# Perceiver layer on one core: the second batch's keys later, one of its head groups in the last cross-attention unit, the last batch's projections one step earlier

## The chip, the cores and the metric

The kernel runs on one core of one Trainium2 chip. The metric is the device time of one execution in microseconds (us). TensorE is called PE here, VectorE DVE, ScalarE ACT, GpSimd POOL, and SyncE, which only issues DMAs, SP.

## What is computed

One layer with three parts, each added to its input `x` of shape (4 batches, 256 tokens, 256): cross-attention to a context of 4096 tokens, causal linear attention over the 256 tokens, and a gated feed-forward network. Biases are left out here:

```python
x = x + cross_attention(layernorm(x), ctx)      # 16 heads of 16, softmax over 4096 keys
x = x + linear_attention(layernorm(x))
x = x + ffn(layernorm(x))

def linear_attention(x):
    q, k, v = split(x @ Wqkv)                   # 16 heads of 16
    qf, kf = features(q), features(k)           # 64 features of a head
    out_t = sum_{s<=t} (qf_t . kf_s) v_s / sum_{s<=t} (qf_t . kf_s)
    return out @ Wout

def features(v):                                # v divided by its norm, then random features
    return exp(clip(omega v/|v| * sqrt(2s) - s, -20, 20)) * weight

def ffn(x):
    return (silu(x @ wg.T) * (x @ wu.T)) @ wd.T
```

Everything is fp32.

## The kernel before

**Cross-attention** (`cross_attention`, L664 to L1137) walks through 16 units, one for each batch and each quad of four heads, and each unit through 16 steps of 256 context tokens. A step `n` issues the score products of its own four heads (`pt`, L845, then the exponentials on ACT, L850), the products of a unit ahead from which the row maxima are taken (`pm` L799, reduced on DVE at L806), then extra pieces of work, and last the value product of step `n - 1` (`pav`, L865), which DVE adds up in `av` (L873, L875). The loop is at L1102. The maxima run 19 steps ahead, so they end in step -4, counted from the first step of the last unit; the key and value projections of the context end before that. In the last unit only `pt`, `pav` and extra pieces are left.

**The extra pieces** come from `plan` (L482), a table by hand. Its keys are steps counted from the start of the last unit: -60 to 11. It holds the causal attention of batches 0, 1 and 2 up to their scaled queries and keys, and the attention of batch 0. `qk_normed(t)` (L277) multiplies the queries and keys of token tile `t` by their inverse norms on DVE. `qk_turned(t)` (L281) turns them with four PE transposes, and DVE copies the result to `qkT`. `features(n)` (L293) makes the features of quads `n` and `n + 1`: PE products `pf` into four PSUM banks, four clamps on DVE (L307), four exponentials on ACT (L308), four scalings on POOL (L309). `normalised` (L158) is a layer norm on DVE alone, 18 instructions for two tiles.

**A quad of the causal attention** is `attend(n)` (L313), three functions called at different places. `scores`: products `pa` (L327, L332) into four banks; two of the four results go to SBUF through an ACT copy (L338) and a POOL select that zeroes the upper triangle (L339), the other two through a DVE product with a mask (L344). `values`: products `po` (L353), copied by ACT (L358). `divide`: for two quads together, PE transposes `pt_o` (L365), then three DVE instructions. Quads 0 to 3 are batch 0, 4 to 7 batch 1, and so on. `output(b)` is the projection after it: transposes `tr_o`, ACT copies, products `py` (L397), DVE adds into `xr` (L398).

**The tail** is the loop over quads at L651. In step `n` it issues `values` of quad `n - 1`, `scores` of quad `n`, `divide` in even steps, `features` where `early` says so, and then `fills[n]`, lists by hand (L594 to L648). The fills hold the feed-forward (`feed_forward`, L536: `turn`, `hidden(0..2)` with the products `pg`, `pu`, and `down` with `pd`) of batch 0 in steps 4 to 8 and of batch 1 from step 9, the end of cross-attention (`divide15`, `project15`), and the causal preparation of batch 3: `norm3`, `turn3`, `qk3` (products `pqk`, DVE add, POOL square), `sq3` (DVE reduce), `v3` (products `pv`, DVE adds), `ends` (the inverse norms, 13 small DVE instructions in five pieces), `qk_normed(6)`, `qk_normed(7)`, `qk_turned(6)`, `qk_turned(7)` and `features(12)`. `begin(1)` is the layer norm of batch 1's feed-forward. `divide15` needs DMAs that `finish(15)` issues on SP after the last `av` (L886 to L904).

**The order** on PE, ACT, DVE and SP is the order of the calls (`manual_schedule`, L591 and L981): each engine works off its own list in turn and waits at its head. All PSUM results come from one ring of eight banks (`bank`, L201), taken in the order of the calls; a product waits until the reader of the result eight allocations ago is done.

Of the kernel before, what the change touches and what calls it, by code (L numbers as in the profile page):

```python
# [12 lines left out]
F32 = mybir.dt.float32  # L13
# [7 lines left out]
P = 128  # L21
B, T, D = 4, 256, 256
# [4 lines left out]
NQ = H // 4  # L27
# [12 lines left out]
def perceiver_layer(  # L40
# [5 lines left out]
    nc = tc.nc  # L46
# [150 lines left out]
    lnp = ctx.enter_context(tc.tile_pool(name="lnp", bufs=2))  # L197
# [79 lines left out]
    def qk_normed(t):  # L277
        to = qk[t].rearrange("p (h d) -> p h d", d=HD)
        nc.vector.tensor_tensor(to, to, nrm[:, t, :].unsqueeze(2).to_broadcast([P, 2 * H, HD]), ALU.mult)

    def qk_turned(t):  # L281
        ps = bank([P, 4, P], "tr_qk")
        for k in range(4):
            nc.tensor.transpose(ps[:, k, :], qk[t][:, k * P : (k + 1) * P], ident)
        nc.vector.tensor_copy(qkT[:, :, t * P : (t + 1) * P], ps)
# [24 lines left out]

    got, place = [], {}

    def attend(n):  # L313

        b, q = divmod(n, NQ)
        ats = []

        def scores():  # L320
            for part in range(2):
                f = feature(n, part)
                qf, kf = f[:, :T], f[:, T:]
                pas = [bank([P, 3, P], "pa") for _ in range(2)]
                for j, pa in enumerate(pas):
                    rows = slice(64 * j, 64 * j + 64)
                    nc.tensor.matmul(  # L327
                        pa[:, 0:2, :], lhsT=kf[rows, :P], rhs=qf[rows, :], start=True, stop=True
                    )
                for j, pa in enumerate(pas):  # L330
                    rows = slice(64 * j, 64 * j + 64)
                    nc.tensor.matmul(  # L332
                        pa[:, 2, :], lhsT=kf[rows, P:], rhs=qf[rows, P:], start=True, stop=True
                    )
                for pa in pas:
                    at = place["at"]()
                    if part == 0:
                        nc.scalar.copy(at, pa)  # L338
                        nc.gpsimd.affine_select(  # L339
                            out=at[:, 0:3:2, :], in_=at[:, 0:3:2, :], compare_op=ALU.is_ge, fill=0.0, base=0,  # L340
                            pattern=[[0, 2], [1, P]], channel_multiplier=-1,
                        )
                    else:
                        nc.vector.tensor_tensor(at, pa, place["mask"], ALU.mult)  # L344
                    ats.append(at)

        def values():
            po = bank([P, T], "po")
            for i in range(2):
                for j, at in enumerate(ats):  # L350
                    c0 = (4 * q + j) * (HD + 1)
                    rhs = at[:, 2, :] if i else at[:, 0:2, :]
                    nc.tensor.matmul(  # L353
                        po[32 * j : 32 * j + 32, i * P : T], lhsT=va[:, 2 * b + i, c0 : c0 + 32], rhs=rhs,
                        start=i == 0, stop=i == 1,
                    )
            oT = place["avT"]()
            nc.scalar.copy(oT, po)  # L358
            got.append(oT)

        def divide():
            pt = bank([P, 2, 8, 32], "pt_o")
            for m, oT in enumerate(got):
                for i in range(2):
                    nc.tensor.transpose(  # L365
                        pt[:, i, 4 * m : 4 * m + 4].rearrange("p j r -> p (j r)"), oT[:, i * P : (i + 1) * P], ident
                    )
            got.clear()
            den = lnp.tile([P, 2, 8], F32, tag="den", name="den")
            nc.vector.tensor_scalar(den, pt[:, :, :, HD], 1e-6, None, ALU.max)  # L370
            nc.vector.reciprocal(den, den)
            nc.vector.tensor_tensor(
                place["att"](b)[:, :, 64 * q - 64 : 64 * q + 64].rearrange("p t (j d) -> p t j d", d=HD),
                pt[:, :, :, :HD], den.unsqueeze(3).to_broadcast([P, 2, 8, HD]), ALU.mult,
            )

        return scores, values, divide
# [54 lines left out]
    def start_causal():  # L432
# [3 lines left out]
        n = 2 * (B - 1)  # L436
# [39 lines left out]
        def call(f, *args):  # L476
            return lambda: f(*args)

        steps = [attend(n) for n in range(NQ)]
        turn_o, project_o = output(0)  # L480
        z0 = lnp.tile([P, 2, D], F32, tag="z1", name="z1", bufs=4)
        plan = {  # L482
# [11 lines left out]
            -13: [call(qk_normed, 0)], -12: [call(qk_normed, 1)],  # L494
            -11: [call(qk_turned, 0)], -10: [call(qk_turned, 1)],
            -7: [call(weight_load, n) for n in range(6)],
            -6: [call(qk_normed, 2)], -5: [call(qk_normed, 3)],
            -4: [call(qk_turned, 2), call(qk_turned, 3), call(weight, 0)],
            -3: [call(features, 0)],
            -2: [call(weight, 1)],  # L500
            -1: [steps[0][0], call(weight, 2)],
            0: [steps[0][1], steps[1][0]],
            1: [call(features, 2)],
            2: [steps[1][1], call(weight, 3), call(qk_normed, 4)],
            3: [steps[1][2], steps[2][0]],
            4: [steps[2][1], steps[3][0]],
            5: [call(weight, 4), call(qk_normed, 5)],
            6: [steps[3][1], call(qk_turned, 4), call(qk_turned, 5)],
            7: [steps[3][2], call(weight, 5)],
            8: [turn_o],  # L510
            9: [call(features, 4)],
            10: [project_o],
            11: [call(normalised, lambda t: z0[:, t, :], (0, 1))],
        }

        for b, at in enumerate((-18, -11, -3)):
# [74 lines left out]
    with tc.manual_schedule(engines={ET.PE, ET.Activation, ET.DVE, ET.SP}):  # L591
        *divide15, project15 = finish
        NB = B * NQ
        fills = {n: [] for n in range(NB + 1)}  # L594
        norm3, turn3, qk3, sq3, v3, _ = causal_in(3)
        ff = {0: feed_forward(0)}

        def call(b, part, *args):
            return lambda: ff[b][part](*args)

        def begin(b):
            ff[b] = feed_forward(b)
            ff[b][0]()

        def outputs(b):
            for piece in output(b):
                piece()


        fills[4] += [call(0, 1)]  # L610
        for m in range(NH // 2):
            fills[5 + m] += [call(0, 2, m)]
        fills[8] += [call(0, 3, i) for i in range(2)]

        fills[6] += divide15
        fills[7] += [project15, norm3]
        turn_o, project_o = output(1)
        fills[8] += [turn_o, turn3, project_o, lambda: begin(1), lambda: qk3(0)]
        ends = normed_pieces((6, 7))
        fills[9] += [lambda: qk3(1), lambda: sq3(0), v3, lambda: sq3(1), *ends[:2]]  # L620
        fills[10] += ends[2:]

        for b in range(1, B):
            n0 = 4 * b + 4
            turn, down = call(b, 1), [call(b, 3, i) for i in range(2)]
            hidden = [call(b, 2, m) for m in range(NH // 2)]
            if b > 1:
                fills[n0] += [lambda b=b: outputs(b)]
                if b == B - 1:
                    fills[n0] += [lambda: nc.scalar.activation(spare, eps, AF.Sqrt)]  # L630
                fills[n0] += [lambda b=b: begin(b)]
            if b < B - 1:
                fills[n0 + 1] += [turn]
                fills[n0 + 2] += [hidden[0]]
            if b < B - 2:
                fills[n0 + 3] += [hidden[1]]
                fills[n0 + 4] += [hidden[2]]
                fills[n0 + 5] += down
            elif b == B - 2:
                fills[n0 + 3] += [hidden[1]]  # L640
                ends = [hidden[2]] + down
            else:
                fills[n0][:0] = ends[:1]
                split = [call(B - 2, 3, 1, parts) for parts in (range(3), range(3, NH))]
                fills[n0] += ends[1:2] + split[:1] + [turn] + split[1:] + hidden + down
        fills[4] += [lambda: features(6)]
        fills[10] += [lambda: qk_normed(6), lambda: qk_normed(7)]
        fills[11] += [lambda: qk_turned(6), lambda: qk_turned(7), lambda: features(12)]  # L648
        early = {6: 8, 8: 10, 13: 14}
        steps = [attend(n) for n in range(NB)]  # L650
        for n in range(NQ, NB + 1):  # L651
            if n > NQ:
                steps[n - 1][1]()
            if n < NB:
                steps[n][0]()
            if n > NQ and n % 2 == 0:
                steps[n - 1][2]()
            if n in early:
                features(early[n])
            for piece in fills[n]:  # L660
                piece()
# [550 lines left out]
```

## Time and profile before

| | us |
|---|---|
| median of 3 runs (1192.37 to 1193.15) | 1193.06 |
| the profiled execution, its own time | 1193.6 |
| its span, first to last instruction | 1191.9 |
| last product of cross-attention starts / the tail's first product | 1064.02 / 1067.26 |
| PE busy, share of the span | 1176.9, 99% |
| DVE busy, share of the span | 912.3, 77% |
| ACT busy, share of the span | 690.7, 58% |

The busy time of PE contains the time that a product stands at the head of its queue with its ends modelled, so 99% does not mean that PE never waits. The waits are read from the chain of work that ended last, and from the idle times ahead of the weight loads (PEld), which stop when PE waits. All times below are us from the start of the span. The last unit begins at 1014.23 (`pt` of step 0).

### The profile page before, as it was taken

To read this page: it belongs to the slowest core of one execution; us is meant where nothing else is said; L and a number is where in the kernel's file an instruction comes from. 1 tells how busy PE (TensorE), PEld (TensorE's weight loads), DVE (VectorE), ACT (ScalarE), POOL (GpSimd) and SP (SyncE) were. 2 spreads that over 40 slices of the span, in tenths; PEclk is the share of its full clock that TensorE was granted. 3 is DMA by queue.
4 is the path that set the end of the run, shared out by engine and by line. 5 is a ranking of instruction groups with operands and counts; after the bars stand their busy time and mean duration, and the time that the engine had idled before them with its cause. 6 is when DMAs were issued, how large, how long until landed. Compare 5 with 4: busy or idle time off the path is not lost.

```text
span 1191.9 us, 43006 instructions
## 1 busy us (share of the span) xinstructions
PE 1176.9 (99%) x18024; PEld 800.7 (67%) x18024; DVE 912.3 (77%) x1756; ACT 690.7 (58%) x1435; POOL 232.5 (20%) x439
## 2 busy tenths in 40 slices
PE   8999999999999999999999999999999999999998
PEld 4476667666776677667766776677666566667677
DVE  7987777877777777877787878798887788557753
ACT  4446666666666666666666666665664446884332
POOL 3730302020211112121212020203021121113210
PEclk8999999999999999999999999999999999999999
DMA  6572432244223322343224322432243120000000
GB/s 209 139 213 72 108 117 81 63 111 118 81 66 96 111 92 83 86 116 94 73 78 117 97 82 77 116 105 73 79 104 89 56 65 28 11 8 9 6 10 18
DMA packets 55161, 100.00 MB, mean 84 GB/s; under 512 B 23392, under 2 KB 28056, under 8 KB 54968
## 3 DMA queue, kind: packets, MB, share of 16 engines
q1 hardware_dynamic: 44904, 91.84, 26.6%
q0 software_dynamic: 9440, 4.81, 2.2%
q8 instruction: 143, 2.34, 0.8%
q10 hardware_dynamic: 624, 0.59, 0.2%
q14 instruction: 50, 0.41, 0.1%
HBM read 76.13 MB, written 3.21 MB: 67 GB/s over the span
## 4 chain that ended last, share of the span: by engine, by line
PE 96%; DVE 2%; ACT 1%; DMA 0%; issue 0%; ACTq 0%; POOL 0%; DVEq 0%
PE pt L845 23%; PE pm L799 19%; PE pav L865 19%; PE pv L180 11%; PE pk L180 11%; PE pg L564 2%; PE pu L564 2%; PE pd L580 1%; PE pa L327 1%; PE pqk L180 1%; DVE mx L806 1%; PE po L353 1%; PE py L397 1%; PE pf L301 1%; PE py L180 1%; PE pa L332 1%
## 5 line engine op out<-in xcount | busy, mean ns | idle before, releaser
L850 ACT ACTIVATE e<-pt 128x512 f32<-128x512 f32 x1024 | 529.8, 602 | 374.0 <-PE pm L799 360.0
L806 DVE TENSOR_REDUCE mx<-pm 128x1 f32<-128x512 f32 x1024 | 634.9, 683 | 124.7 <-PE pm L799 124.4
L845 PE MATMUL pt<-qa,kt 32*128 32x256 f32 x4096 | 504.1, 388 | 0.9 <-DVE qa L831 0.5
L799 PE MATMUL pm<-kt,qT 32*128 32x512 f32 x2048 | 501.9, 617 | 0.1
L845 PEld LDWEIGHTS pt<-qa,kt 32*128 32x128 f32 x4096 | 319.3, 184 | 124.3 <-ACT v L770 41.6
L865 PE MATMUL pav<-e,v 128*32 128x256 f32 x4096 | 269.9, 380 | 0.0
L799 PEld LDWEIGHTS pm<-kt,qT 32*128 32x128 f32 x2048 | 183.2, 191 | 17.6 <-DVE mx L806 4.9
L865 PEld LDWEIGHTS pav<-e,v 128*32 128x32 f32 x4096 | 128.7, 110 | 76.1 <-issue 5.6
L875 DVE TENSOR_TENSOR av<-pav,av 128x256 f32<-128x256 f32 x240 | 101.6, 423 | 62.2 <-PE pav L865 61.9
L180 PE MATMUL pv<-wv_sb,wff 128*32 128x128 f32 x4096 | 137.3, 276 | 0.0
L180 PE MATMUL pk<-wff,wk_sb 128*32 128x256 f32 x2048 | 137.1, 389 | 0.0
L180 PEld LDWEIGHTS pv<-wv_sb,wff 128*32 128x32 f32 x4096 | 104.3, 109 | 43.9 <-DVE mx L806 43.9
L180 PEld LDWEIGHTS pk<-wff,wk_sb 128*32 128x32 f32 x2048 | 54.7, 110 | 66.6 <-DVE mx L806 38.8
L914 POOL TENSOR_TENSOR oT<-oT,bvT 128x64 f32<-128x64 f32 x32 | 8.6, 289 | 391.0 <-DVE oT L911 391.0
L897 POOL DMA_DIRECT2D oT<-scr x112 | 66.5, 623 | 21.3 <-DMA scr<-av 18.3
L742 ACT ACTIVATE ku<-pk,bk_sb 128x256 f32<-128x256 f32 x128 | 63.2, 495 | 12.6 <-PE pk L180 11.1
L821 POOL DMA_DIRECT2D qa<-neg x60 | 33.0, 559 | 141.5 <-DVE neg L818 104.4
L770 ACT COPY v<-pv 128x256 f32<-128x256 f32 x128 | 51.3, 401 | 9.7 <-PE pv L180 9.7
L308 ACT ACTIVATE kt<-kt,shift 128x512 f32<-128x512 f32 x32 | 22.3, 727 | 18.1 <-DVE kt L307 18.1
L972 POOL DMA_DIRECT2D qT<-qu x56 | 26.9, 488 | 15.3 <-ACT qu L969 10.7
L344 DVE TENSOR_TENSOR at<-pa,mask 128x384 f32<-128x384 f32 x32 | 16.3, 551 | 16.0 <-PE pa L332 15.9
L307 DVE TENSOR_SCALAR kt<-pf,low,top 128x512 f32<-128x512 f32 x32 | 23.7, 803 | 5.0 <-PE pf L301 5.0
(143 smaller groups left out, 646.0 us busy)
## 6 DMA issues: line engine op xcount, KB each, us to landing
wff<-in_ctxT_dram SPq DMA_DIRECT2D x128, 512.0 KB
kt<-ku SPq DMA_DIRECT2D x510, 32.0 KB
scr<-av POOLq DMA_DIRECT2D x14, 128.0 KB, 2.0
oT<-scr POOLq DMA_DIRECT2D x112, 8.0 KB, 2.5
xr<-in_x_dram SPq DMA_DIRECT2D x4, 256.0 KB
out_dram<-o SPq DMA_DIRECT2D x8, 128.0 KB
qa<-neg POOLq DMA_DIRECT2D x60, 1.0 KB, 3.4
qT<-qu POOLq DMA_DIRECT2D x56, 16.0 KB, 3.8
```

What stands on the lines that cost most here:

```text
L180: nc.tensor.matmul(out[js], lhsT=lhsT[:, js], rhs=rhs, **flags)
L564: nc.tensor.matmul(ps[:, i, :], lhsT=w[:, k, ns], rhs=zT[:, k, :], start=k == 0, stop=k == KC - 1)
L742: nc.scalar.activation(ku[:, cs], made.pop(), AF.Identity, bias=bk_sb[:, m : m + 1])
L770: nc.scalar.copy(to.rearrange("p t (h d) -> p t h d", d=HD + 1)[:, :, :, :HD], made.pop().rearrange("p t (h d) -> p t h d", d=HD),)
L799: nc.tensor.matmul(pm, lhsT=qT[rows, q, ts], rhs=kt[rows, c * CH : (c + 1) * CH], start=True, stop=True,)
L806: nc.vector.tensor_reduce(mx[:, i, j, c : c + 1], pm, AX.X, ALU.max)
L821: nc.gpsimd.dma_start(out=qa[32 * j : 32 * j + 1, :].rearrange("o (p i) -> o p i", i=2), in_=neg[:, j, :])
L845: nc.tensor.matmul(pt[:, i, :], lhsT=kt[rows, ks], rhs=qa[rows, :], start=True, stop=True)
L850: nc.scalar.activation(e, pt, AF.Exp, scale=0.25)
L865: nc.tensor.matmul(pav[32 * h : 32 * h + 32, :], lhsT=v[:, t % KT, c0 : c0 + 32], rhs=es[n, h][:, i, :], start=i == 0, stop=i == 1,)
L875: nc.vector.tensor_tensor(avs[u], pav, avs[u], ALU.add)
L897: queue.dma_start(out=oT[:, k, q % 2, j], in_=scr[32 * j : 32 * j + HD, k * P : (k + 1) * P].rearrange("e (r a) -> r e a", a=16),)
```

## The change

It does four things. (1) In `plan`, `qk_normed` and `qk_turned` of tiles 2 and 3 (batch 1) leave steps -6 to -4 and take the places that tiles 4 and 5 (batch 2) had in steps 2, 5 and 6; tiles 4 and 5 go to steps 8, 11, 13 and 14. (2) Quad 4, the first of batch 1, has its `scores` in step 12 and its `values` in step 15 of the last unit and not in steps 4 and 5 of the tail; with `scalar=False` all four of its results go through DVE's mask, and DVE copies its `po` into a tile of its own. (3) `divide15` goes ahead of `divide` of quads 4 and 5 in step 6, `project15` and `norm3` from step 7 to step 6, `turn3` from 8 to 7, `qk3` from 8 and 9 to 8 alone, with the first ahead of `down` and the second ahead of `project_o`, and `ends` all to step 9. (4) `qk_turned(6)` goes to the end of step 10, and `qk_turned(7)` and `features(12)` go ahead of `hidden(1)` of batch 1 in step 11.

```diff
-    def attend(n):
+    def attend(n, scalar=True):
...
-                    if part == 0:
+                    if part == 0 and scalar:
                         nc.scalar.copy(at, pa)
...
                     else:
                         nc.vector.tensor_tensor(at, pa, place["mask"], ALU.mult)
...
-            oT = place["avT"]()
-            nc.scalar.copy(oT, po)
+            if scalar:
+                oT = place["avT"]()
+                nc.scalar.copy(oT, po)
+            else:
+                oT = lnp.tile([P, T], F32, tag="avT4", name="avT4", bufs=1)
+                nc.vector.tensor_copy(oT, po)
             got.append(oT)
...
-        steps = [attend(n) for n in range(NQ)]
+        steps, step4 = [attend(n) for n in range(NQ)], attend(NQ, False)
...
-            -6: [call(qk_normed, 2)], -5: [call(qk_normed, 3)],
-            -4: [call(qk_turned, 2), call(qk_turned, 3), call(weight, 0)],
+            -4: [call(weight, 0)],
...
-            2: [steps[1][1], call(weight, 3), call(qk_normed, 4)],
+            2: [steps[1][1], call(weight, 3), call(qk_normed, 2)],
...
-            5: [call(weight, 4), call(qk_normed, 5)],
-            6: [steps[3][1], call(qk_turned, 4), call(qk_turned, 5)],
+            5: [call(weight, 4), call(qk_normed, 3)],
+            6: [steps[3][1], call(qk_turned, 2), call(qk_turned, 3)],
             7: [steps[3][2], call(weight, 5)],
-            8: [turn_o],
+            8: [turn_o, call(qk_normed, 4)],
             9: [call(features, 4)],
             10: [project_o],
-            11: [call(normalised, lambda t: z0[:, t, :], (0, 1))],
+            11: [call(normalised, lambda t: z0[:, t, :], (0, 1)), call(qk_turned, 4)],
+            12: [step4[0]],
+            13: [call(qk_normed, 5)],
+            14: [call(qk_turned, 5)],
+            15: [step4[1]],
...
-        fills[6] += divide15
-        fills[7] += [project15, norm3]
+        first = {6: divide15}
+        fills[6] += [project15, norm3]
+        fills[7] += [turn3]
         turn_o, project_o = output(1)
-        fills[8] += [turn_o, turn3, project_o, lambda: begin(1), lambda: qk3(0)]
+        fills[8][:0] = [lambda: qk3(0)]
+        fills[8] += [turn_o, lambda: qk3(1), project_o, lambda: begin(1), lambda: sq3(0)]
         ends = normed_pieces((6, 7))
-        fills[9] += [lambda: qk3(1), lambda: sq3(0), v3, lambda: sq3(1), *ends[:2]]
-        fills[10] += ends[2:]
+        fills[9] += [v3, lambda: sq3(1), *ends]
...
-        fills[10] += [lambda: qk_normed(6), lambda: qk_normed(7)]
-        fills[11] += [lambda: qk_turned(6), lambda: qk_turned(7), lambda: features(12)]
+        fills[10] += [lambda: qk_normed(6), lambda: qk_normed(7), lambda: qk_turned(6)]
+        fills[11][:0] = [lambda: qk_turned(7), lambda: features(12)]
...
         for n in range(NQ, NB + 1):
-            if n > NQ:
+            if n > NQ + 1:
                 steps[n - 1][1]()
-            if n < NB:
+            if NQ < n < NB:
                 steps[n][0]()
+            for piece in first.get(n, []):
+                piece()
             if n > NQ and n % 2 == 0:
                 steps[n - 1][2]()
```

## The prediction

> **What bounds the kernel now.** I read the chain of waits first: 96% of it is PE, so work taken off PE or waits ahead of PE decide. Then the busy times of the stretches that the edits touch:
>
> ```profile
> 985.00:1002.33 17.33, 17.33 (x196) 10.30 (x193) 16.84 (x37) 10.43 (x20) 0.54 (x2) 1.00 0.15 48
> ...
> 1014.23:1051.00 36.77, 36.77 (x503) 23.97 (x503) 18.91 (x43) 32.12 (x66) 6.03 (x14) 1.00 0.05 9
> 1051.00:1067.26 16.26, 15.91 (x199) 8.56 (x198) 7.95 (x30) 13.13 (x26) 1.69 (x5) 1.00 0.01 3
> ...
> 1104.20:1131.20 27.00, 24.40 (x256) 17.14 (x248) 21.62 (x59) 8.38 (x17) 5.92 (x11) 1.00 0.01 2
> ```
>
> The columns after the length are PE, PEld, DVE, ACT, POOL, granted clock (1.00 throughout). Unit 14 (first row) is DVE's: 16.84 of 17.33. The last unit is PE's with ACT close behind. In the tail's middle (last row) DVE is busy for 21.62 of 27.00 and PE is short of work for some of it. So the change moves DVE work out of a stretch that DVE bounds, PE work from the tail into the last unit, and reorders a stretch in which PE and DVE take turns.
>
> **Unit 14: the pieces that leave.** The timeline there:
>
> ```profile
> 995.65 0.68 DVE L279 TENSOR_TENSOR kt<-kt,nrm 128x512 f32<-128x512 f32 x1
> 996.25 0.41 DVE L875 TENSOR_TENSOR av<-pav,av 128x256 f32<-128x256 f32 x1
> ...
> 999.18 0.68 DVE L279 TENSOR_TENSOR kt<-kt,nrm 128x512 f32<-128x512 f32 x1
> ...
> 1001.31 1.09 PE L284 MATMUL tr_qk<-ident,kt 128*128 128x128 f32 x8
> ...
> 1002.50 1.27 DVE L285 COPY qT<-tr_qk 128x512 f32<-128x512 f32 x2
> 1003.70 0.41 DVE L875 TENSOR_TENSOR av<-pav,av 128x256 f32<-128x256 f32 x1
> ```
>
> Start to start, the two scalings hold DVE for 0.60 each and the copies for 1.20: 2.40, and DVE has no idle time there. PE loses 1.0 of transposes. A step cannot fall below what PE needs: `pav` starts at 984.10 and 987.02, 2.92 apart, in the step without extras. The steps -5 and -4 now last 3.73 and 4.55 (`pav` at 994.05, 997.78, 1002.33). Following the queues, `pav` of -5 comes 0.60 earlier (DVE), that of -4 3.0 after it, at 1000.2 for 1002.33: **-2.1**. Ends: -0.9 if PE sets the pace in spite of the busy DVE, -2.4 if all of DVE's time is won. The new row maximum of the last unit comes earlier by as much, so its four POOL DMAs (issued from 1005.56) still land ahead of 1014.23 as they do now. Steps 2, 5 and 6 get tiles 2 and 3 for tiles 4 and 5, the same instructions: nothing.
>
> **The last unit: what is added.** PE: two `qk_turned` of 0.59, `scores` 1.51 (1032.37 to 1033.88), `values` 0.79 (1031.59 to 1032.37): 3.48. DVE: two scalings 0.68, two copies 0.69, four masks of 0.51, one copy of 0.42 (as L873): 5.2. ACT gets nothing. In the end of the unit PE waits twice:
>
> ```profile
> 1058.41 0.34 DVE av L875
> 1058.76 0.04 issue
> 1058.80 1.13 PE pt L845 x12
> 1059.94 1.00 PE pav L865 x16
> ...
> 1064.09 3.25 PE pav L865 x32
> ```
>
> `pt` of step 13 (first four at 1057.75, the rest at 1058.80) waits 1.05 for the bank that `av` frees behind `normalised`; the last two `pav`, 1.0 each, take 3.25: 1.25 of waiting for ACT. Now step by step. `qk_normed(4)` in step 8 falls in 2.24 of DVE idle ahead of 1046.24: free. In step 11 `qk_turned(4)` takes 0.59 of PE, and its copy goes behind `normalised`, to 1059.0. In step 12 PE reaches the second half of `scores` at 1057.95; its two banks are the ones of that copy and of step 11's `av` (1059.35), so it waits 1.1. The masks behind run to 1061.4; `pt` of step 13 needs the first one's bank only at 1061.1. So the old wait is replaced by one of the same size. `values` in step 15 falls in the wait for ACT's last exponentials and uses it up. 3.48 + 1.1 - 1.05 - 1.25 = 2.3; laid out bank by bank it comes to **+2.5**. Ends: +1.2 (3.48 less both waits), +4.5 (each added DVE wait is paid by PE: 1.1 again in step 13 and 0.9 in step 14).
>
> [...]
>
> **The tail.** I count from the end of the last `pav`, 1067.26 now. PE has 2.3 less to do (`pa`, `po` of quad 4). The waits now are at 1101.07 (0.7, ACT's `oT`) and here:
>
> ```profile
> 1124.98 1.21 DVE qT L285 x2
> 1126.18 0.14 issue
> 1126.32 1.15 PE pf L301 x16
> 1127.47 0.80 DVE kt L307
> 1128.30 0.73 ACT kt L308
> 1129.03 0.09 issue
> 1129.12 0.49 POOL kt L309
> 1129.61 0.04 issue
> 1129.65 0.70 PE pa L327 x4
> ```
>
> That is 1.2 ahead of `features(12)` and 1.4 ahead of quad 12, 3.3 in all. If PE ran through, quad 12's `pa` would start at 62.4 - 2.3 - 3.3 = 56.8 and not 62.4. But DVE is in the way three times.
>
> (a) `norm3`. PE: `tr_z` 0.59, `pf` 1.07, `pa` 1.51, `pg`/`pu` 3.65, `po` 0.79, `pa` 1.51 end at 9.1; masks to 10.2. The last DMA for `divide15` is issued at 1075.14 and bytes flow until 1077.9, 10.6 on this count, so DVE may wait some 0.5. Then, start to start: reciprocals and product 1.2 (1086.18 to 1087.37), `divide` 0.82, clamps up to the gate 4.24 (1080.54 to 1084.78, with ACT's exponentials between), gate 1.4, `xr` 0.35, `normalised` 4.5 (1091.50 to 1096.00): 12.5, to 22.7. PE reaches `turn3` at 9.1 + 0.59 + 1.07 + 3.65 + 1.0 + 0.79 + 1.51 + 3.65 = 21.4 and waits 1.3. Next, `values(7)` needs masks that stand on DVE behind `norm3`: 23.7, so `po` ends at 24.3.
> (b) From there PE runs: `pa` 1.51, `pt_o` 0.59, `pf` 1.07, `pqk` 1.85, `pd` 5.38, `tr_o` 0.59, `pqk` 1.85, `py` 1.99, to 39.1. `begin(1)` follows on DVE at 39.5; now it starts at 1104.16, 36.9. DVE is then full: `normalised` 4.5, `sq3` 0.67, masks 1.0, `v3` 0.7, `sq3` 0.7, `ends` 3.2, masks 1.0, `divide` 0.82, gate 1.4, first scaling 0.65: 14.6, to 54.1. PE's own work up to there is 10.8, to 49.9; it waits 4.2 in parts, ahead of `turn`, of `values(9)` and most of all of `qk_turned(6)`.
> (c) `tr_qk` 0.5, `po` 0.8, `pa` 1.5, `tr_qk` 0.5 to 57.4; the copy behind the masks of quad 11 to 58.1; `pf` to 59.3, `hidden(1)` 3.66, `po` 0.79: `pa` of quad 12 at 63.7. The clamps are hidden under `hidden(1)`, as now they are not.
>
> 63.7 for 62.4 is +1.3, and four handoffs between engines, 0.04 to 0.14 each in the rows, bring **+1.8**. Behind quad 12 the lists are the same. Ends: -5.6 (PE runs through), +3.0 (1.2 more if the DMA lands at 12 and all of (a) shifts). Parts of the fill that cost nothing do so under PE products: the clamps of `features(10)` under `pqk` and `pd` (7.2), the output copies under the second `pqk`.
>
> **Sum:** -2.1 + 2.5 + 1.8 = +2.2 on the profiled execution, 1193.6 (span 1191.9 and 1.7 around it): 1195.8. The median of the runs lies 0.5 lower: **1195.3**. About 0.2%, 2.4 us, can be told from no change, so the forecast lies on the edge.
>
> **Rivals.** *A, faster: PE runs through the tail.* It needs DVE 1.3 earlier at `turn3` and 4 earlier at `qk_turned(6)`. For it: PE loses 2.3 of work, and the waits at 1126 and 1129 are covered. Against it: DVE's 21.62 of 27.00, and its list at each of the three places. In full -2.1 + 2.5 - 5.6 = -5.2, 1187.9; half of it 1190.5. *B, slower: the last unit's masks hold the banks.* Steps 11 to 14 give DVE 10.7 us of work in about 12; if the masks end 1.2 later than I put them, `pt` of step 13 waits too and PE pays +4.5: 1197.3. Against it: only that slack of 1.2. *C, the relief of unit 14 does not come*, because PE sets its pace: -0.9 for -2.1, 1196.5. For it: the step of 2.92; against it: no idle time on DVE.
>
> **Chances.** Forecast 0.50 (own range 1193.4 to 1197.2; within 0.24, slower 0.26); A 0.20 (faster 0.16, within 0.04); B 0.15 (slower); C 0.15 (within 0.04, slower 0.11). Faster 0.16, within 0.2% 0.32, slower 0.52. The range leaves out half of A and the far end of B: 1190.0 to 1198.6.
>
> **What would show it.** Right: `pav` of step -4 some 2 us earlier against that of -6; `pa` of quad 4 split by a wait near 1 us, and no gap between the last two `pav`; from the last `pav` to `pa` of quad 12 about 64; a wait ahead of `turn3` and a larger one ahead of `tr_qk` of tile 6, both for DVE. Wrong: PE without waits from quad 8 to quad 12 (then A), `pt` of steps 13 and 14 waiting for DVE (then B), or `pav` of -5 and -4 where they were (then C).

## The result, and the profile after

| | before | after |
|---|---|---|
| median of 8 runs each, us | 1193.18 | 1196.54 (1196.29 to 1198.02) |
| ratio, with its 95% interval | | 1.0031 [1.0021, 1.004] |
| span of the profiled execution | 1191.9 | 1194.7 |
| end of the last `pav` of cross-attention | 1067.33 | 1068.09 |
| from there to `pa` of quad 12 | 62.3 | 64.6 |
| from `pa` of quad 12 to the end | 62.25 | 62.02 |

The change costs 0.3%. Busy times hardly move: on the page of the profile after, PE has 1177.0, DVE 914.2, ACT 689.2. The shares of the chain of waits by engine tell more, before and after:

```profile
PE 96%; DVE 2%; ACT 1%; DMA 0%; issue 0%; ACTq 0%; POOL 0%; DVEq 0%
...
PE 94%; DVE 4%; ACT 1%; issue 0%; POOL 0%; DVEq 0%; ACTq 0%; POOLq 0%
```

The chain has lost two points of PE, of 96. So no engine got more to do; DVE carries more of the chain. That is not yet a wait of PE, which can work beside it (from 982.90 to 1000.04 PE is busy for 17.14 us and DVE for 16.35); where PE stands, the stretches tell.

**Unit 14.** The timeline of the changed kernel, PE, the `pav` of steps -6 and -4 (start, length):

```profile
993.93 1.07 PE L874 MATMUL pav<-e,v 128*32 128x256 f32 x16
...
1000.04 1.07 PE L874 MATMUL pav<-e,v 128*32 128x256 f32 x16
```

They were at 994.05 and 1002.33, with -5 at 997.78 (997.05 now). From -6 to -4 it is 6.11 now and was 8.28: 2.17 won. Both steps last about 3 us now, the pace of the steps without extra pieces.

**The last unit.** Its timeline in step 12, with the idle time ahead and its releaser in brackets:

```profile
1056.04 0.69 DVE L285 COPY qT<-tr_qk 128x512 f32<-128x512 f32 x1
1056.64 0.42 DVE L884 TENSOR_TENSOR av<-pav,av 128x256 f32<-128x256 f32 x1
...
1056.87 0.72 PE L327 MATMUL pa<-kt 64*128 64x256 f32 x3 [1.08 <-DVE qT L285]
...
1057.96 1.07 PE L874 MATMUL pav<-e,v 128*32 128x256 f32 x16
```

`scores` of quad 4 is cut in two. The second half waits from 1055.73 to 1056.87, 1.14, for the bank that DVE's copy `qT` frees; the second bank is free only after `av`, at 1057.06, and the half takes 1.16 by the chain (1056.87 to 1058.03) where it needs 0.65 (1070.61 to 1071.26, in the tail). That is 1.6 of waiting. The `pt` of steps 13 and 14 behind it follow without a gap. The last `pav` ends 0.76 later than before although unit 14 handed over 2.17 (and the trace up to there 0.12) earlier: the last unit costs 3.05.

**The tail**, in the chain of waits of the changed kernel (start, length, engine, tile, line):

```profile
1065.63 2.46 PE pav L874 x32
...
1077.26 0.78 DVE at L344 x2
...
1089.74 0.42 DVE z L172
...
1090.30 0.67 PE tr L224 x4
1090.97 1.33 PE po L353 x15
...
1104.99 1.94 PE py L401 x8
...
1121.72 0.61 DVE kt L279
...
1122.47 0.63 PE tr_qk L284 x4
...
1125.44 1.00 DVE at L344 x2
1126.44 0.61 DVE qT L285
...
1127.10 1.15 PE pf L301 x16
...
1132.68 0.63 PE pa L327 x4
```

The chain leaves PE three times: at the masks at 1077.26, to come back at the end of `norm3` (`z`, ahead of `turn3`, at 1090.30); at the output of batch 1 (`py`, then the DVE adds into `xr` at 1106.95), from where DVE alone carries the chain for 15.4 us until it has scaled the first piece of tile 6 (`kt`, to 1122.33); and at the masks and the copy ahead of `features(12)`. Before, it left PE for 10.6 us from `norm3` to `py` (1091.15 to 1101.79) and then only around `features(12)`. PE's own waits up to quad 12 are now 0.97 ahead of `turn3`, 0.59 ahead of `turn` of batch 1's feed-forward, 2.56 ahead of tile 6 and 1.12 ahead of `features(12)`, 5.2 in all; before they were 0.7 ahead of `py`, 1.2 ahead of `features(12)` and 1.4 ahead of quad 12, 3.3 in all. Two value products (`po`) that wait for masks in their middle come on top: 1.33 and 1.92 for 0.79. So the PE products that quad 4 took with it, and the waits that went, are lost in PE's waits for DVE, the largest of them for tile 6. Sum: -0.12 - 2.17 + 3.05 + 2.27 - 0.23 = +2.8, the difference of the spans.

### The profile page after: what moved, and what is told of

The parts are those of the page before. It is cut to its first block, busy times and chain, and to the rows that moved or that the text cites. A ratio compares the mean times of both kernels' runs of the same rounds, so it can differ in the third digit from the quotient of the medians.

```text
span 1194.7 us, 43006 instructions
## 1 busy us (share of the span) xinstructions
PE 1177.0 (99%) x18024; PEld 800.8 (67%) x18024; DVE 914.2 (77%) x1759; ACT 689.2 (58%) x1432; POOL 231.2 (19%) x437
## 4 chain that ended last, share of the span: by engine, by line
PE 94%; DVE 4%; ACT 1%; issue 0%; POOL 0%; DVEq 0%; ACTq 0%; POOLq 0%
PE pt L854 23%; PE pm L808 19%; PE pav L874 19%; PE pv L180 11%; PE pk L180 11%; PE pd L587 2%; PE pg L571 1%; PE pu L571 1%; PE pqk L180 1%; PE pa L327 1%; DVE mx L815 1%; PE po L353 1%; PE py L401 1%; PE pf L301 1%; PE py L180 1%; PE pa L332 0%
## 5 line engine op out<-in xcount | busy, mean ns | idle before, releaser
L884 DVE TENSOR_TENSOR av<-pav,av 128x256 f32<-128x256 f32 x240 | 101.6, 423 | 57.8 <-PE pav L874 57.5
L180 PEld LDWEIGHTS pk<-wff,wk_sb 128*32 128x32 f32 x2048 | 54.7, 110 | 66.6 <-DVE mx L815 38.8
L981 POOL DMA_DIRECT2D qT<-qu x56 | 26.8, 486 | 14.4 <-ACT qu L978 11.5
L307 DVE TENSOR_SCALAR kt<-pf,low,top 128x512 f32<-128x512 f32 x32 | 23.7, 804 | 5.6 <-PE pf L301 5.6
```

What stands on the lines that cost most here:

```text
L180: nc.tensor.matmul(out[js], lhsT=lhsT[:, js], rhs=rhs, **flags)
L884: nc.vector.tensor_tensor(avs[u], pav, avs[u], ALU.add)
L981: nc.gpsimd.dma_start(out=qT[r0 : r0 + HD, 2 * m + h // 4, b * T : (b + 1) * T], in_=qu[h * HD : (h + 1) * HD, :])
```

## The experiments

My theory after the result: the moved keys and quad 4 are a gain; the new order of the tail (part 3) loses it, because it puts `norm3`, `begin(1)` and `ends` on DVE's list in such an order that PE waits for tile 6; part 4 is neither. Rivals: part 4 loses by itself; the last unit loses; PE's own order, not DVE's list, makes the waits.

### Parts alone

**Part 1 alone** (the keys' places in `plan`; quad 4 stays in the tail).

> Part (1) of the change alone: the scalings and turns of tiles 2 to 5 later, all else as before. Theory (the prediction's terms): unit 14 gives back 2.2 us, the two turns of tiles 4 and 5 cost PE 1.2 in the last unit, the tail is as before: 1.0 faster, 1192.2. Rival C (PE sets unit 14's pace): 0.9 - 1.2, no change. Rival B (DVE's added copies hold banks in the last unit): 1.0 to 1.5 slower.

Measured: 0.9995 [0.9986, 1.0004], 1192.66. The runs show no difference that can be told; the interval, -1.7 to +0.5 us, also holds the theory's -1.0. The profile shows the theory's terms. From its chain, the `pav` of step -6 and the last ones:

```profile
992.87 1.07 PE pav L866 x16
...
1061.94 3.25 PE pav L866 x32
1065.18 0.63 PE pa L327 x4
```

From the one to the end of the other it is 72.3 for 73.3 before: the 2.17 of unit 14 less 1.2 for two turns more in the last unit.

**Parts 1 and 2** (the tail's old order; the loop without quad 4):

```diff
+            12: [step4[0]],
+            15: [step4[1]],
...
-            if n > NQ:
+            if n > NQ + 1:
                 steps[n - 1][1]()
-            if n < NB:
+            if NQ < n < NB:
                 steps[n][0]()
```

> Parts (1) and (2): quad 4 attended in the last unit, the tail's order otherwise as before. Theory (the tail's new order is what loses): the last value product ends 0.8 later than before, as in the changed kernel, and the tail is 1.7 shorter because PE has 2.3 less to do: 0.9 faster, 1192.3. Rival (DVE sets the tail's length, so taking quad 4 out of it gains nothing there, and the new order costs nothing): 0.8 to 1.0 slower, 1194.1. Rival (the loss is the last unit's): 3 slower.

Measured: 0.9986 [0.9977, 0.9995], 1191.44. From the chain of waits:

```profile
1068.09 0.59 PE tr_z L562 x4
...
1128.12 0.70 PE pa L327 x4
```

The last unit ends where that of the changed kernel does, at 1068.09, and quad 12 comes 60.0 behind it: with the old order the tail keeps all of the 2.3 that quad 4 took off PE.

**Parts 3 and 4** (the tail's order, with quad 4 in the tail):

> Parts (3) and (4) alone: the tail's new order with quad 4 still in the tail, the plan as before. Theory: DVE's list sets turn3, qk3 and qk_turned(6) as in the changed kernel, now 2.3 later less 0.5 of waiting for the DMA: 4.0 slower, 1197.2. Rival (the order costs nothing): within 1 of before.

Measured: 1.0044 [1.0031, 1.0056], 1198.93; I expected 4.0 more than before and by the medians it was 5.8. -1.4 and +4.4 per mille of the two halves give +3.0; the whole change has +3.1. So the halves add up, within some 1 per mille of each, and the loss is in the tail's order. That they add up so closely is partly luck, for this kernel loses by a falling clock that the profile of the changed kernel does not show. The 1.8 that I had not expected show in the busy times of the stretches around the first turn of tile 6 (columns: window, length, PE, PEld, DVE, ACT, POOL, granted clock, DMA):

```profile
1121.00:1123.60 2.60, 0.47 (x3) 0.06 (x1) 2.46 (x6) 0.00 (x0) 0.00 (x0) 1.00 0.01 3
...
1125.60:1127.00 1.40, 1.40 (x12) 1.22 (x10) 0.00 (x0) 0.37 (x1) 0.00 (x0) 0.50 0.05 12
```

PE does 0.47 of 2.60 while it waits, and behind that the granted clock is 0.50, with 0.69 and 0.70 in the stretches next to it (1123.60 to 1125.60 and 1127.00 to 1128.30). `po` takes 1.38 there instead of 0.79. Two later experiments return to this.

**Part 4 alone:**

```diff
-        fills[11] += [lambda: qk_turned(6), lambda: qk_turned(7), lambda: features(12)]
+        fills[10] += [..., lambda: qk_turned(6)]
+        fills[11][:0] = [lambda: qk_turned(7), lambda: features(12)]
```

> Part (4) alone: qk_turned(6) at the end of step 10, qk_turned(7) and features(12) ahead of hidden(1). Theory: the first turn waits 1.4 for DVE's scaling, and the waits of 1.2 and 1.4 around features(12) go; quad 12 starts where it did: within 0.5 of before. Rival (this reorder is what loses, for the turn of tile 6 now stands ahead of PE work that covered it): 1.7 to 2.5 slower.

Measured: 1.0004 [0.9995, 1.0012], 1193.31: nothing, as expected.

**The whole change without part 4:**

> The changed kernel with part (4) undone: hidden(1) again ahead of qk_turned(6), qk_turned(7) and features(12). Alone, part (4) cost nothing. Theory: with part (3) it costs, since DVE's scaling of tile 6 comes 4.7 after PE could turn it, and hidden(1) would fill 3.7 of that. Quad 12 starts some 3 earlier than in the changed kernel: 1193.5, level with before. Rival (part (3) costs all of it by itself): as the changed kernel, 1196.5. Rival (part (4) covers the clamps and so gains): 1 to 2 slower than the changed kernel.

Measured: 1.0008 [0.9999, 1.0017], 1195.07. Quad 12 comes 63.1 behind the last `pav` for 64.6; I expected twice that gain. The chain says why:

```profile
1127.48 1.21 DVE qT L285 x2
...
1132.15 0.70 PE pa L327 x4
```

`features(12)` stands behind two copies again and quad 12 right behind its own features, as before the change: the two old waits are back. Part 4 does avoid them; with part 3 ahead of it, it only brings PE to the wait for tile 6 earlier. So my theory on part 4 holds only without part 3. From parts 1 and 2 (0.9986) the ratio rises to 1.0008 with part 3 and to 1.0031 with part 4 on top: each brings about half of the loss.

### The tail's order, piece by piece

**`begin(1)` ahead of both `qk3`:**

```diff
-        fills[8][:0] = [lambda: qk3(0)]
-        fills[8] += [turn_o, lambda: qk3(1), project_o, lambda: begin(1), lambda: sq3(0)]
+        fills[8] += [turn_o, project_o, lambda: begin(1), lambda: qk3(0), lambda: qk3(1), lambda: sq3(0)]
```

> The changed kernel with both qk3 behind begin(1) in step 8, as they were before relative to it; turn3 stays in step 7. Theory: begin(1)'s layer norm on DVE starts 2.5 to 3 earlier, the two pqk run under it, but their bias adds now stand behind it on DVE (1.2); tile 6 is scaled 1 to 2 earlier and quad 12 as much: 1195.3. Rival (the wait at turn3 behind norm3 is what loses): no change against the changed kernel, 1196.5.

Measured: 1.0024 [1.0015, 1.0033], 1196.42. Tile 6 is turned 52.6 behind the last `pav` for 54.4, 1.8 earlier as expected, but quad 12 gains only 0.4. The busy times around the turn:

```profile
1117.00:1119.50 2.50, 0.00 (x0) 0.00 (x1) 2.04 (x5) 0.00 (x0) 0.00 (x0) 0.96 0.01 3
1119.50:1121.00 1.50, 1.47 (x12) 0.94 (x16) 0.83 (x2) 0.00 (x0) 0.00 (x0) 0.50 0.00 0
```

PE is idle for 2.5 us and then runs for 3.2 us at a clock of 0.50 (in windows of 0.1 us the clock is 0.50 from 1119.3 to 1122.7). It does half as much in it: 12 matmuls in 1.50, where the changed kernel has 22 in the stretch that begins with the same turn.

**The same order, with PE kept busy:** 14 products ahead of the first turn of tile 6.

```diff
+        warm = lambda: [nc.tensor.matmul(ps, lhsT=ident, rhs=ident, start=True, stop=True)
+                        for ps in [bank([P, P], "warm2")] for _ in range(14)]
+        fills[10] += [warm, lambda: qk_turned(6)]
```

> The order in which begin(1) goes ahead of both qk3, with 14 products of 128x128 more, into a bank that nobody reads, ahead of the first turn of tile 6, where PE otherwise waits 2.5 us. Theory (the fall of the granted clock to 0.50 behind that wait comes from the idle time): the granted clock stays near 1.00 there, po of quad 10 takes 0.79 for 1.44, tr_qk of tile 6 0.63 for 1.08, and pa of quad 12 comes 1.2 to 1.4 earlier, 63.0 after the last pav for 64.2; ratio about 1.0013. Rival (the fall has nothing to do with that wait): clock and durations as without the fillers, 64.2, ratio 1.0024.

Measured: 1.0011 [1.0002, 1.002], quad 12 at 63.2. The stretch with the turn:

```profile
1121.20:1122.50 1.30, 1.30 (x23) 0.77 (x22) 0.69 (x1) 0.00 (x0) 0.00 (x0) 1.00 0.05 13
```

The clock stays at 1.00, ahead of it and up to 1126.80 too, `po` takes 0.79 (1.44), and quad 12 comes 1.1 earlier although the fillers, 3.1 us in all, push the turn back by 0.6. The runs agree: 7 of the 11 without fillers have a mean granted clock below 0.997, none of the 11 with them. So in this order the fall of the clock comes from the idle time.

**No masks on DVE for quads 7, 9 and 10:**

```diff
-                    if part == 0 and scalar:
+                    if (part == 0 or n in (7, 9, 10)) and scalar:
                         nc.scalar.copy(at, pa)
```

> The changed kernel with all four results of quads 7, 9 and 10 through ACT's copy and POOL's select, none through DVE's mask. Theory (DVE's in-order list sets when tile 6 can be turned): two masks of 0.5 leave DVE behind norm3 and four ahead of the scaling of tile 6; values(7) no longer stands behind norm3, though turn3 still does, and the first tr_qk of tile 6 comes 2 to 2.5 us earlier than 54.4 after the last pav; quad 12's first pa at 62.3 to 63.0 instead of 64.6; ratio to before about 1.001 to 1.0015. Rival (the order of PE's own list sets it, the masks are covered): pa of quad 12 at 64.6, ratio 1.003. Second rival (ACT and POOL become late instead: two copies and two selects more for each quad): values(7), (9) or (10) wait for POOL, pa of quad 12 later than 64.6.

Measured: 1.0006 [0.9997, 1.0015], 1194.56. PE's timeline:

```profile
1120.18 0.63 PE L284 MATMUL tr_qk<-ident,kt 128*128 128x128 f32 x4 [1.79 <-DVE kt L279]
...
1121.53 1.02 PE L327 MATMUL pa<-kt 64*128 64x256 f32 x4
```

With four masks less ahead of it on DVE, tile 6 is turned at 52.3 for 54.4: the 2 to 2.5 of the theory. `po` of quad 7 ends at 23.7 for 24.2. Quad 12 gains only 0.8 in the profiled execution (63.8; expected 62.3 to 63.0): `pa` takes 2.70 in all for 1.51, at a granted clock of 0.53, once more behind an idle PE. The runs spread from 1193.31 to 1195.88. The rival with ACT and POOL late is out: no chain goes through their copies and selects there, and the time fell. DVE's in-order list is what PE waits for. The medians gain more than the profiled execution shows, 2.0 of the 2.1 at the turn. The clock explains it as far as is known: the profiled execution, 1195.45, is the only one of the 11 with a mean granted clock below 0.997 (0.996).

**`turn3` one step later**, at the head of step 8.

> The changed kernel with turn3 at the head of step 8, behind values(7) and pa of quad 8, and not at the end of step 7. Theory (PE's wait there is for DVE's list: values(7) needs masks that stand behind norm3, so it waits as long wherever turn3 stands): the end of po of quad 7 moves by at most 0.4 from 24.2 after the last pav, quad 12 within 0.4 of 64.6, ratio 1.003. Rival (turn3's place on PE is the cause): po of quad 7 ends 1.3 earlier, at 22.9, quad 12 at 63.3, ratio 1.002.

Measured: 1.0072 [1.0059, 1.0085], 1202.44: neither theory. `po` of quad 7 ends at 24.45 for 24.2, so the first half of the theory holds: the masks behind `norm3` make that wait, not `turn3`. But quad 12 comes at 69.9. DVE's timeline:

```profile
1096.80 2.96 DVE L307 TENSOR_SCALAR kt<-pf,low,top 128x512 f32<-128x512 f32 x4
1099.67 0.68 DVE L225 COPY zT<-tr 128x512 f32<-128x512 f32 x1
```

The copy of `turn3`'s result, `zT`, now stands behind quad 8's masks, `divide` and the four clamps of `features(10)`, and `qk3` waits for it until 1100.40: 31.4 behind the last `pav`, 27.4 in the changed kernel. All the 4.0 arrive at tile 6 (58.4 for 54.4), and the clock falls behind that wait too. I had followed PE's list and forgotten that the moved piece has a copy that moves on DVE's.

### What is better than both

**Quad 4 one step later in the last unit**, in the kernel of parts 1 and 2:

```diff
-            8: [turn_o, call(qk_normed, 4)],
+            8: [turn_o, call(qk_normed, 4), call(qk_normed, 5)],
...
-            11: [call(normalised, ...), call(qk_turned, 4)],
-            12: [step4[0]],
-            13: [call(qk_normed, 5)],
+            11: [call(normalised, ...)],
+            12: [call(qk_turned, 4)],
+            13: [step4[0]],
```

> Run e2 with quad 4's scores in step 13, qk_turned(4) in step 12 and both scalings of tiles 4 and 5 in step 8. Theory: the 1.5 that the scores wait in step 12 are DVE's list behind the layer norm of step 11; one step later PE finds the banks free. The last value product ends 1.3 earlier than in e2: 1190.1. Rival (the masks themselves hold the banks, wherever they stand): as e2, 1191.4.

Measured: 0.997 [0.9959, 0.9982], 1190.34. From its chain of waits:

```profile
1055.36 1.70 PE pt L852 x16
1057.06 0.63 PE pa L327 x4
...
1058.57 1.00 PE pav L872 x16
```

`scores` runs through in 1.51, but `pt` ahead of it takes 1.70 for 1.08: it waits 0.6 for an `av` behind the same layer norm. The last unit ends at 1066.55 for 1068.09 in the kernel of parts 1 and 2. Of this 1.54, the trace up to step -6 brings 0.58 (its `pav` is at 993.35 for 993.93), and 0.96 is won behind it: the wait of 1.6 that went, less the 0.6. The medians give 1.1.

**In addition**, tiles 6 and 7 turned ahead of `hidden(1)` and `features(12)` put inside it, between its two products, in the old order of the tail:

```diff
+                fills[n0 + 3] += [
+                    lambda: qk_turned(6), lambda: qk_turned(7),
+                    lambda: made.extend(ff[1][4](1)), lambda: made.pop(0)(),
+                    lambda: features(12), lambda: made.pop(0)(),
+                ]
```

> e7, and in step 11 of the tail: qk_turned(6) and (7) ahead of hidden(1), and hidden(1) cut in two, pg with its gate ahead of features(12) and pu behind it. Theory: the copies of tiles 6 and 7 hide under pg, the clamps under pu; the two waits around features(12), 1.3 and 1.4, go: 2.5 faster than e7, 1187.6. Rival (DVE's list is what sets quad 12, as in the changed kernel): no gain over e7, 1190.1.

Measured: **0.9959 [0.9946, 0.9971]**, 1188.68, faster than both kernels. Its chain has no step of another engine there (1121.82 to 1124.53 are `pu` and `po`):

```profile
1117.99 1.02 PE tr_qk L284 x8
1119.01 1.73 PE pg L575 x8
1120.74 1.08 PE pf L301 x16
...
1124.53 0.63 PE pa L327 x4
```

Quad 12 comes 57.5 behind the last `pav` for 60.0 without this edit, the 2.5 of the theory; the medians show 1.7 of it. The copies of the tiles run under `pg` (1118.98 to 1120.26), the clamps of the features under `pu` and `po` from 1122.01, and the exponentials (from 1122.85) and scalings (from 1123.67) under these and quad 12's first `pa`. This is what the change's parts 3 and 4 reach for, without touching `norm3`, `qk3` and `begin(1)`.

## Why the prediction was right, and where it was off

- **Unit 14: right.** -2.1 predicted, -2.17 measured, and both steps fall to the pace of about 3. Rival C, with no relief, is out.
- **The last unit: mechanism right, size off**, +2.5 for +3.05. The step that was mis-sized is the wait of `scores`: "it waits 1.1" was the first bank's wait, measured at 1.14. I named the second bank too, that of step 11's `av`, but let it count nothing; it comes after the copy and adds 0.5. "The wait for ACT's last exponentials", which `values` was to use up, left 0.46 of 1.25, so the sign "no gap between the last two `pav`" failed. From `pav` to `pav`, the sum 3.48 + 1.1 - 1.05 - 1.25 = 2.3 came out as 3.48 + 1.6 - 1.2 - 0.8 = 3.1. The old wait of step 13 is gone and `pt` of steps 13 and 14 do not wait, as predicted; so rival B, whose decisive point that was, is out, though the time came nearer to its 1197.3 than to the forecast. That the wait was worth removing, the kernel with quad 4 in step 13 shows: 0.96 back.
- **The tail: right in its mechanism**, +1.8 predicted, +2.27 measured. Point by point, counted from the last `pav`: `po` of quad 7 ends at 24.3 predicted, 24.2 measured; `py` at 39.1 and 38.8; tile 6 turned at 54.1 and 54.4; PE's wait ahead of `turn3` 1.3 and 0.97. The 0.5 that DVE might wait for the DMA in `divide15` did not come: the two reciprocals follow the masks without idle time at 1078.18 and take 0.95, as in the kernel before. The mis-sized term is (c): `pf` of `features(12)` was put to end at 59.3 and ended at 60.2, because the copy ahead of it stands behind both masks of quad 11 (1.0, from the end of the last `pa`), of which I had let only a part count; my 0.5 for handoffs covered about half of it.
- **Rival A**, PE running through, did not happen, for the reason given against it, DVE's list at its three places. The runs show this reason twice: with DVE's masks taken out of the list the turn of tile 6 comes 2.1 earlier, with one copy put further down in it 4.0 later. Its size was real: the kernel with `hidden(1)` split has quad 12 at 57.5, and 56.8 was my figure for a PE without waits.
- **The sum**, +2.2, was 0.6 short of the profiled difference of +2.8, which is 0.55 in the last unit and 0.47 in the tail, less 0.23 behind quad 12 and less 0.2 up to the end of unit 14. The price list was right in the two places where I followed the lists of both engines in order, and short where I took a wait for several banks as a wait for the first. By the medians the change costs 3.4, and the 1196.5 is to the tenth the figure of rival C: the time alone could not have told the forecast from B and C; the rows do.

Not settled: how much of the runs' spread of the changed kernel (1196.29 to 1198.02) is a falling clock. In its profiled execution the clock stayed at 1.00 behind the wait for tile 6. Of the eight runs, only the slowest has a mean granted clock below 0.997 (0.996). The kernel before spreads by 3.0 us (1192.03 to 1195.03 in one series) and none of the 70 with a clock on record is below 0.997. A run at 0.997 can still hold a fall: the profiled execution with `begin(1)` first does.

## What to carry to other kernels

In a kernel whose engines work off lists in order, moving a piece moves each of its instructions on each engine's list: price it by what it now stands behind and what now stands behind it (4.0 us for one copy, with `turn3` late), and where a product needs several banks, by the last one freed (1.6 for 1.1, in step 12). An average of DVE's load, 77% of the span before and after, says nothing of this; a layer norm of 18 small instructions is a block of 4.2 to 4.6 us (`norm3` from 1086.17 to 1090.39, `begin(1)` from 1107.30 to 1111.85 in the changed kernel) for all that is queued behind it. To fill a wait, put work of the waiting engine between two pieces that are already there (the two products of `hidden(1)`), rather than pull the chain that it waits for ahead of others.

## What the runs showed of the hardware that I had not expected

In four of the kernels a wait of PE cost more than its length: PE idle for 1.8 to 2.6 us ahead of tile 6 was followed by a granted clock of 0.50 (parts 3 and 4 alone, `begin(1)` first, masks off DVE, `turn3` late). In windows of 0.1 us it lasts 3.4 us in each of the four (with the masks off DVE, the stretches have a mean clock of 0.53 for 2.60 us and 0.73 for 1.80, which is the same), and it begins between 0.2 us before the end of the gap and 1.6 us after it. Quad 12 then comes 11.5 to 11.9 us after the turn of tile 6, for 10.2 in the changed kernel: 1.2 to 1.6 more. With 14 unread products in the gap it did not happen. Half the clock for 3.4 of 1195 us takes 0.0014 off a run's mean clock; runs below 0.997 are found only in these four, in the changed kernel and with part 4 alone: 3 of 5 for parts 3 and 4, 2 of 11 for part 4 alone, 7 of 11 for `begin(1)` first, 1 of 11 with the masks off DVE, 4 of 5 for `turn3` late, 1 of 8 for the changed kernel. With part 4 alone the wait ahead of tile 6 is only my estimate, 1.4. It does not follow every such gap: in the changed kernel itself the idle time is 2.56 in the profiled execution, as long as in the kernel with `begin(1)` first, and the clock there stayed at 1.00:

```profile
1120.00:1122.40 2.40, 0.00 (x0) 0.00 (x0) 1.95 (x4) 0.00 (x0) 0.00 (x0) 1.00 0.01 3
1122.40:1123.90 1.50, 1.43 (x22) 0.93 (x22) 1.21 (x2) 0.00 (x0) 0.00 (x0) 1.00 0.00 0
```

Why one wait of 2.56 was followed by the fall and an equal one was not, no run shows.
